# Six graph layers on one core: seven products for layer 2's queries, late copies of turned rows, one product moved, and thirteen stores on another queue

## The chip, the cores and the metric

The kernel runs on one core of a Trainium2 chip. The metric is the time of one execution on the device in microseconds (us), the median of several runs. One execution was also recorded by the hardware profiler; its records give a line, an engine, a start and a duration for every instruction. Durations quoted here come from that one execution. PE is the matrix engine, DVE the vector engine, ACT the scalar engine, POOL is GpSimd, and SP is the engine that issues most transfers. A queue such as SPq is the sequencer of an engine[...].

## The reference

A graph has N = 3327 nodes with 256 features each and a dense 0/1 adjacency matrix. Four residual layers are applied, each followed by a layer norm; the fourth holds three attention layers, which makes six stages in the kernel. Cut to what matters:

```python
# layer 0: cosine attention
Qn = cos_normalize(x @ Wq.T); Kn = cos_normalize(x @ Wk.T)
att = softmax(where(adj > 0, Kn @ Qn.T, NEG), axis=1)
x = layernorm(x + 0.5 * mask_of_empty_rows(att @ x, x) + 0.5 * x)
# layer 1: graph attention (GAT)
h = x @ W
e = leaky_relu(h @ a[:D] + (h @ a[D:]).T)
x = layernorm(x + elu(softmax(where(adj > 0, e, NEG)) @ h))
# layer 2: dot-product attention
q, k, v = x @ Wq.T + bq, x @ Wk.T + bk, x @ Wv.T + bv
x = layernorm(x + elu(softmax(where(adj > 0, q @ k.T / 16, NEG)) @ v))
# layer 3: h = x @ W0, then three GAT layers (3a, 3b, 3c), residual, layernorm
```

The adjacency matrix masks every attention. The kernel holds the weights transposed: a tile e has 128 nodes that are looked at on the partitions and 512 nodes that look along the columns, and the sum over neighbours is a matrix product that accumulates over the 26 row tiles.

## The kernel before

The nodes are padded to 3328, which is NT = 26 tiles of 128 rows. The columns fall into NB = 7 blocks: six of 512 columns (four tiles) and a last one of 256 (two tiles). The work is one long list of steps (layer, block b, tile j), 26 x 7 steps for each of the six layers in the order 0, 1, 2, 3a, 3b, 3c. Layers 1, 3a, 3b and 3c are GAT layers.

**A step.** `make` creates the weights of a step three steps ahead (`make_to`, LA): ACT computes an exponential or the two parts of the leaky form, DVE multiplies by the mask, and the result is the tile `e`. Then PE multiplies the e tile with the values of tile j and accumulates in `po`, which takes four PSUM banks for a full block and two for the last. A plain step does this with one 257-column product for each column tile (L1432). A block for which `strassen` is true (layer 2, and blocks 1 to 5 of layer 0) takes its steps in pairs and uses seven half-size products in place of eight; `sums` makes four combinations of the two e tiles on DVE, `combine` makes four combinations of the values once for each pair and stores them in DRAM (L713, through SP's queue), and `fetch_tsum` loads them again.

**The end of a block.** `finish` is a generator in `pending`; `advance()` takes it one step forward in each of the following steps, so that the end of block b is interleaved with the beginning of block b+1. In a GAT layer it scales the rows (`p4`, L1026), and `turn` (L827) transposes them: ACT separates the 32-bit rows into two planes of 16-bit halves (L834), SP issues one transposing DMA, the generator lets some steps pass (`turn_steps`, L848), and DVE copies the two planes back into place (L844). Then PE projects the rows with the weights of the layer (`pproj`, L1062), and exponential linear unit, residual and layer norm follow. The blocks before the last but one are projected by `projected4`, which uses seven products too, with four combined weights in `wsum`, spare columns of `FT[NB - 1]`. So the separate products of L1062 are found only in blocks NB-2 and NB-1. The scaled values of block NB-2 are turned during the last block, and those of the last block during the first steps of the next layer.

**The queries of layer 2.** `block2(b)` (L515) multiplies the transposed features of block b with a 256x256 matrix G (four 512-column products L522 in two `pgq` banks), adds a bias on ACT (L529), and takes a bound of the scores: a reduction on DVE (L537) and the product `pn` over the partitions (L545). The main loop starts it ahead of the block through `pre = ahead(nl, nb)` at step `begin` = 14 and takes it forward once a step. So block 0 of layer 2 is prepared in the last steps of layer 1, and it needs the rows that `finish` has just made.

**What sets the order.** The instructions are written in one program order. A scheduler that is entered at the start and closed after the first steps orders what each engine gets, by data dependence and by its own costs; every engine then runs its list in order. Tiles come from pools with a fixed number of buffers: e has five, `tsums` three, the tag `stage` (adjacency rows, turned planes, p4, x4) four, and the small PSUM pool for ps, pgq, pproj, pv and pn has three banks. An instruction that takes a buffer waits for its former readers.

**Layer 0, block 0** also reads the adjacency matrix as 32-bit numbers (L424), turns it into masks (ACT L435, L436), counts rows (DVE L449, L460; PE `pasum` L464), and normalises the keys of the next block on POOL (`kss`, `rs_*`, `rk`, L308 and L137 to L160), whose result DVE L379 and ACT L390 use. The thirteen stores of L713 for layer 0 fall into it.

The line of the plain product, before the change:

```python
for k in range(len(pos)):
    nc.tensor.matmul(pos[k], es[:, k * P : (k + 1) * P],
                     V[L.i % 2][j], start=(j == 0), stop=(j == NT - 1))
```

Of the kernel before, what the change touches and what calls it, by code (L numbers as in the profile page):

```python
# [8 lines left out]
F32 = mybir.dt.float32  # L9
# [4 lines left out]
AF = mybir.ActivationFunctionType  # L14
ALU = mybir.AluOpType
# [4 lines left out]
P = 128  # L20
D = 256
H = 128
# [11 lines left out]
def gnn_stack(ctx: ExitStack, tc: tile.TileContext, a: dict, N: int, out: bass.AP):  # L34
# [8 lines left out]
    nc = tc.nc  # L43
    NT = (N + P - 1) // P
    NP = NT * P
    NB = (NP + CH - 1) // CH
# [3 lines left out]
    def bw(b):  # L50
        return min(CH, NP - b * CH)
# [7 lines left out]
    cols = ctx.enter_context(tc.tile_pool(name="cols", bufs=2))  # L59
    mpool = ctx.enter_context(tc.tile_pool(name="mpool", bufs=2))  # L60
    work = ctx.enter_context(tc.tile_pool(name="work", bufs=2))
# [4 lines left out]
    def bank(name):  # L66
# [4 lines left out]
    start = tc.manual_schedule(  # L71
        engines={engines.PE, engines.Activation, engines.DVE, engines.Pool}
    )
# [9 lines left out]
    n = 8  # L83
# [9 lines left out]
    for k in range(4):  # L93
# [5 lines left out]
    V = [  # L99
        [big.tile([P, D + 1], F32, name=f"v{i}_{t}") for t in range(NT)]  # L100
        for i in range(2)
    ]

    FT = [big.tile([P, 2, CH], F32, name=f"ft{g}") for g in range(NB)]
# [6 lines left out]
    t_d = {  # L111
        k: [dram.tile([P, 4 * H + 1], F32, name=f"t{k}_d{p}") for p in range(NT // 2)]
        for k in ("0", "2")
    }
# [397 lines left out]

    gq = {}

    def block2(b):  # L515

        wd = bw(b)
        g = work.tile([P, 2, CH], F32, tag="x4k", name="gT", bufs=2)
        for o in range(2):
            pm = bank("pgq")  # L520
            for h in range(2):
                nc.tensor.matmul(  # L522
                    pm[:, :wd],
                    w["G"][:, h, o * P : (o + 1) * P],
                    FT[b][:, h, :wd],
                    start=(h == 0),
                    stop=(h == 1),
                )
            nc.scalar.activation(  # L529
                g[:, o, :wd], pm[:, :wd], AF.Identity, bias=w["u"][:, o : o + 1]  # L530
            )
            yield

        gm = cols.tile([P, 2], F32, tag="gm", name="gm")
        nc.vector.tensor_reduce(  # L537
            gm, g[:, :, :wd], AX.X, ALU.max, apply_absolute_value=True
        )
        nc.vector.tensor_tensor(gm, gm, gm, ALU.mult)  # L540
        g1 = cols.tile([P, 1], F32, tag="g1", name="g1")
        nc.vector.tensor_tensor(g1, gm[:, 0:1], gm[:, 1:2], ALU.add)
        yield
        pn = bank("pn")
        nc.tensor.matmul(pn[:, :1], ones, g1, start=True, stop=True)  # L545
        yield
        n2 = cols.tile([P, 1], F32, tag="n2", name="n2")
        nc.vector.tensor_scalar(n2, pn[:, :1], TINY, None, ALU.max)
        off = cols.tile([P, 1], F32, tag="off", name="off")
        rsqrt(off, n2, 1)  # L550
        nc.vector.tensor_tensor(off, off, n2, ALU.mult)
        nc.vector.tensor_scalar(off, off, -1.0, 80.0, ALU.mult, ALU.add)
        nc.vector.tensor_scalar(off, off, 0.0, None, ALU.min)
        gq[b] = g, off
# [135 lines left out]
    def combine(key, p, v, e=None):  # L690


        b1, b2 = v[2 * p], v[2 * p + 1]
        b11, b12, b21, b22 = b1[:, H:D], b1[:, :H], b2[:, H:D], b2[:, :H]
        if (key, p) in kept or key == "0":
            t = work.tile([P, 4 * H + 1], F32, tag="tsum", name="tsums", bufs=3)
        else:
            t = work.tile([P, 4 * H + 1], F32, tag="x4k", name="tsum", bufs=2)
        if (key, p) in kept:
            tsums[kept[key, p], p] = t  # L700
        t1, t2, t3, t4 = (t[:, c : c + H] for c in (0, H + 1, 2 * H + 1, 3 * H + 1))
        if e is None:
            nc.gpsimd.memset(t[:, H : H + 1], 1.0)
            nc.vector.tensor_tensor(t1, b12, b11, ALU.subtract)
            nc.vector.tensor_tensor(t3, b22, b12, ALU.subtract)
        else:
            one = t[:, H : H + 1]
            nc.vector.tensor_scalar(one, e[:, :1], 0.0, None, ALU.is_ge)
            nc.vector.scalar_tensor_tensor(t1, b12, one, b11, ALU.mult, ALU.subtract)
            nc.vector.scalar_tensor_tensor(t3, b22, one, b12, ALU.mult, ALU.subtract)  # L710
        nc.vector.tensor_tensor(t2, b22, t1, ALU.subtract)
        nc.vector.tensor_tensor(t4, t2, b21, ALU.subtract)
        nc.sync.dma_start(t_d[key][p], t)  # L713

    def fetch_tsum(key, b, p):
        t = work.tile([P, 4 * H + 1], F32, tag="tsum", name="tsums", bufs=3)
# [107 lines left out]
        return z[:, : 2 * q]  # L824


    def turn(x4, n, out, steps=3):  # L827

        half = "p k (n t) -> p t k n"
        pl = work.tile([P, 4, 2, D], U16, tag="x4k", name="planes", bufs=2)
        for t in range(2):
            nc.scalar.copy(pl[:, :n, t, :], x4[:, :n, :].bitcast(U16).rearrange(half, t=2)[:, t])  # L834
        yield
        tr = work.tile([P, 16, P], U16, tag="stage", name="turned", bufs=4)
        nc.sync.dma_start_transpose(
            out=tr[:, : 4 * n, :], in_=pl[:, :n].rearrange("p k t n -> p (k t n)")
        )
        for _ in range(steps):  # L840
            yield
        trv = tr[:, : 4 * n, :].rearrange("p (k t h) i -> p t k h i", t=2, h=2)
        for t in range(2):
            nc.vector.tensor_copy(out(t), trv[:, t])  # L844
        yield

    def turn_steps(L, b):

        if L.key == "1":
            return 5 if b == NB - 2 else 3  # L850
        return (9 if L.key == "3c" else 7) if b == NB - 2 else 4

    wsum = [
        FT[NB - 1][:, i // 2, D + (i % 2) * H : D + (i % 2 + 1) * H] for i in range(4)
    ]

    def sum_weights(wt):  # L860
        b11, b12, b21, b22 = (wt[:, h, o * H : (o + 1) * H] for h in range(2) for o in range(2))
# [72 lines left out]
    def finish(L, b, pos):  # L934
# [76 lines left out]
        else:  # L1011
# [25 lines left out]
            if L.key != "2":  # L1037
                pT4 = work.tile([P, 4, 2, P], F32, tag="x4k", name="pT4", bufs=2)
                yield from turn(
                    p4,  # L1040
                    n,
                    lambda t: pT4[:, :n].bitcast(U16).rearrange(
                        "p k h (i t) -> p t k h i", t=2
                    )[:, t],
                    turn_steps(L, b),
                )
                pTs = {k: pT4[:, k] for k in range(n)}
                if b < NB - 2:
                    c4 = work.tile([P, 4, D], F32, tag="x4k", name="c4", bufs=2)
                    yield from projected4(pT4, w[L.w], c4)  # L1050
# [304 lines left out]
    for s, (L, b, j) in enumerate(steps):  # L1355
# [43 lines left out]
        if end:  # L1399

            k, h = divmod(2 * j, NT)
            for i in (h, h + 1):
                for o in range(2 if k else 1):
                    e = made[i][:, k * P : (k + 1) * P]
                    nc.tensor.matmul(  # L1405
                        pos[1 + o][:, :P] if k else pos[0],
                        V[1][i][:, o * H : (o + 1) * H] if k else e,
                        e if k else V[1][i],
                        start=(i == 0),
                        stop=(i == NT - 1),  # L1410
                    )
            if j == 0:
                xm = fetch_last()

            if j == 9:
                esum = work.tile([P, D], F32, tag="ejunk", name="esum", bufs=2)[:, :P]
                nc.vector.tensor_tensor(esum, made[0][:, P:D], made[1][:, P:D], ALU.add)
            elif 9 < j < 22:
                for i in (2 * j - 18, 2 * j - 17):
                    nc.vector.tensor_tensor(esum, esum, made[i][:, P:D], ALU.add)  # L1420
            elif j == 23:
                pn = bank("pnlast")
                nc.tensor.matmul(pn[:, :1], esum, ones[:, :1], start=True, stop=True)
                rlast = cols.tile([P, 1], F32, tag="ri3", name="ri3")
                row_sums(pn[:, :1], rlast)
            if j == NT // 2 - 1:
                ends.append(finish_last(pos[0], xm, 0))
            if ends:
                next(ends[0], None)
        elif not strassen(L, b):  # L1430
            for k in range(len(pos)):
                nc.tensor.matmul(  # L1432
                    pos[k],
                    es[:, k * P : (k + 1) * P],
                    V[L.i % 2][j],
                    start=(j == 0),
                    stop=(j == NT - 1),
                )
        elif j % 2:
            products(pos, b, j // 2, es, V[L.i % 2])  # L1440
# [24 lines left out]
        if nb == NB:  # L1465
            nl, nb = (None if last else layers[L.i + 1]), 0
        begin = 2 if last and b == NB - 2 else 14
        if L.is_gat and (b, j) == (0, 22):
            sum_weights(w[L.w])
        if j == (25 if L.key == "1" else 22) and not end:  # L1470
# [87 lines left out]
```

## Time and profile before

| | us |
|---|---|
| median of 3 runs | 2356.33 (2355.39 to 2357.3) |
| the profiled execution, whole | 2355.78 |
| its span, first to last record | 2354.0 |
| one full block of layer 2 (905 to 994) | 89.0, of which DVE busy 56.9, ACT 22.6 |

The profiled execution is 0.55 us under the median, and 1.78 us of it lie outside the span. On PE every product leaves two records, so that a count of records is twice the count of products. The durations of single PE records overlap; what a product costs is the distance from start to start. In the stretches without waits that distance is, for one record, 0.429 us at 512 columns, 0.217 at 257, 0.216 at 256 and 0.112 at 128 or 129, and so for a product 0.858, 0.433, 0.431 and 0.223 us.

A line of the timeline gives start, length, engine, line, operation, names and the number of records that were merged. In brackets is the idle time of the engine ahead of it and what ended that.

### The profile page before, as it was taken

The page shows a single profiled execution, that of the slowest core. Times are in us where ns is not written, and L with a number is a line of the kernel's source. Part 1 is how long each engine was busy: PE and PEld are TensorE (multiplying, and loading weights), DVE is VectorE, ACT ScalarE, POOL GpSimd, SP SyncE. Part 2 cuts the span into 40 slices and gives each one's busy share as a digit, 9 for nine tenths or more (in the row PEclk, how much of TensorE's full clock was granted, in tenths as well). Part 3 has the DMA queues.
Part 4 walks back from the last instruction along what each step waited for, and adds up shares of the span by engine and source line. Part 5 has one row for each costly group of instructions (what it writes and reads, how often), then busy time and mean ns, then how long its engine had stood idle before and what let it go on. Part 6 is the DMA issues. An engine that isn't in the chain of part 4 may idle for free.

```text
span 2354.0 us, 33990 instructions
## 1 busy us (share of the span) xinstructions
PE 2335.3 (99%) x12257; PEld 1917.4 (81%) x12257; DVE 1665.8 (71%) x4500; ACT 1221.5 (52%) x1976; POOL 40.0 (2%) x156
## 2 busy tenths in 40 slices
PE   9999999999999999999999999999999999999997
PEld 6788888888888777767677798888888888888887
DVE  7789999867777666567567586666756666666676
ACT  4667777755555422222222255565665555655554
POOL 0000000000000000000000000000000000000000
PEclk9999999999999999999999999999999999999999
DMA  8655555423222312212212221210211111132111
GB/s 275 196 187 184 167 199 191 151 75 83 74 81 60 108 54 88 79 54 86 76 46 74 83 88 48 73 56 26 71 53 43 43 51 52 50 101 70 61 44 46
DMA packets 147293, 214.72 MB, mean 91 GB/s; under 512 B 76093, under 2 KB 101172, under 8 KB 142516
## 3 DMA queue, kind: packets, MB, share of 16 engines
q1 hardware_dynamic: 146852, 212.28, 28.1%
q8 instruction: 96, 1.57, 0.3%
q14 instruction: 73, 0.60, 0.1%
q10 hardware_dynamic: 272, 0.26, 0.0%
HBM read 167.53 MB, written 28.19 MB: 83 GB/s over the span
## 4 chain that ended last, share of the span: by engine, by line
PE 94%; DVE 3%; ACT 1%; DMA 1%; issue 1%; POOL 0%; SPq 0%; POOLq 0%; DVEq 0%; ACTq 0%
PE po L1432 48%; PE po L779 19%; PE ps L563 12%; PE ps L492 6%; PE pproj L890 3%; PE po L1405 1%; PE pv L1148 1%; PE pgq L522 1%; ACT re L657 1%; DMA stage<-in_adj_a 1%; PE pk L353 0%; DMA turned<-planes 0%; PE pq L317 0%; DVE e L668 0%; PE pproj L1062 0%
## 5 line engine op out<-in xcount | busy, mean ns | idle before, releaser
L1432 PE MATMUL po<-v,e 128*128 128x257 f32 x5616 | 1248.6, 381 | 1.5 <-ACT p L1026 1.3
L1432 PEld LDWEIGHTS po<-v,e 128*128 128x128 f32 x5616 | 1057.7, 190 | 165.3 <-issue 9.3
L657 ACT ACTIVATE re<-u,nrh,th 128x512 f32<-128x512 f32 (+1 forms) x728 | 556.1, 780 | 483.9 <-DVE e L668 478.0
L668 DVE SCALAR_TENSOR_TENSOR e<-re,rh,mask 128x512 f32<-128x512 f32 (+1 forms) x702 | 501.2, 718 | 347.6 <-PE po L1432 311.6
L563 PE MATMUL ps<-gT,ft 128*128 128x512 f32 (+1 forms) x728 | 307.4, 563 | 0.0
L571 ACT ACTIVATE ex<-ps,off 128x512 f32<-128x512 f32 (+1 forms) x182 | 119.1, 655 | 356.6 <-PE ps L563 356.0
L779 PE MATMUL po<-tsums,ssum 128*128 128x128 f32 (+1 forms) x1794 | 249.3, 275 | 0.0
L477 DVE SCALAR_TENSOR_TENSOR e<-ex,mask 128x512 f32<-128x512 f32 (+1 forms) x182 | 118.6, 651 | 164.1 <-ACT ex L571 163.3
L563 PEld LDWEIGHTS ps<-gT,ft 128*128 128x128 f32 x728 | 132.0, 190 | 114.5 <-issue 111.7
L779 PEld LDWEIGHTS po<-tsums,ssum 128*128 128x128 f32 x1794 | 224.5, 192 | 0.7 <-ACT y L982 0.3
L779 PEld LDWEIGHTS po<-v,e 128*128 128x128 f32 x1196 | 169.3, 191 | 67.4 <-issue 54.7
L779 PE MATMUL po<-v,e 128*128 128x129 f32 x1196 | 182.4, 275 | 0.0
L505 ACT ACTIVATE ex<-ps,rq 128x512 f32<-128x512 f32 (+1 forms) x183 | 118.7, 651 | 116.8 <-PE ps L492 107.5
L492 PE MATMUL ps<-ft,ft 128*128 128x512 f32 (+1 forms) x312 | 142.5, 561 | 0.0
L506 DVE SCALAR_TENSOR_TENSOR e<-ex,mask 128x512 f32<-128x512 f32 (+1 forms) x183 | 116.8, 644 | 34.2 <-ACT ex L505 33.2
L449 DVE CUSTOM_DVE_ANT_0 acc<-acc,stage 128x1024 uint16<-128x1024 uint16 (+1 forms) x168 | 108.7, 647 | 12.3 <-DMA stage<-in_adj_a 9.2
L779 PE MATMUL po<-tsums,e 128*128 128x128 f32 x598 | 92.3, 275 | 0.4 <-DVE y L821 0.4
L779 PE MATMUL po<-v,ssum 128*128 128x128 f32 x598 | 92.3, 275 | 0.0
L436 ACT ACTIVATE mask<-pos 128x1024 uint8<-128x1024 bf16 (+1 forms) x87 | 86.4, 993 | 2.1
L435 ACT ACTIVATE pos<-stage 128x1024 bf16<-128x1024 int32 (+1 forms) x87 | 85.6, 984 | 1.2 <-DVE e L506 1.2
L779 PEld LDWEIGHTS po<-tsums,e 128*128 128x128 f32 x598 | 79.3, 192 | 0.6 <-issue 0.6
L779 PEld LDWEIGHTS po<-v,ssum 128*128 128x128 f32 x598 | 79.4, 192 | 0.1
(295 smaller groups left out, 1899.7 us busy)
## 6 DMA issues: line engine op xcount, KB each, us to landing
mask<-mask_d SPq DMA_DIRECT2D x30, 1664.0 KB
stage<-in_adj_a SPq DMA_DIRECT2D x78, 512.0 KB
tsums<-t_d SPq DMA_DIRECT2D x152, 256.5 KB
mask_d<-mask SPq DMA_DIRECT2D x6, 1664.0 KB
u<-s_d SPq DMA_DIRECT2D x24, 256.0 KB
xT<-in_xT SPq DMA_DIRECT2D x10, 512.0 KB
mask<-mask_d SPq DMA_DIRECT2D x5, 832.0 KB
t_d<-tsums SPq DMA_DIRECT2D x14, 256.5 KB
```

The lines of the kernel that those rows point to most:

```text
L436: nc.scalar.activation(mask(b, j, 2), t_[:, : 2 * wd], AF.Sign)
L449: nc.vector.tensor_tensor(acc, acc, st[:, h * wd : (h + 1) * wd], ALU.add)
L477: nc.vector.scalar_tensor_tensor(e[:, :wd], t_[:, :wd], 0.0, mask(b, j), ALU.add, ALU.mult)
L492: nc.tensor.matmul(ps[:, :wd], FT[j // 4][:, 0, (j % 4) * P : (j % 4 + 1) * P], FT[b][:, 1, :wd], start=True, stop=True,)
L505: nc.scalar.activation(t_[:, c], ps[:, c], AF.Exp, scale=rq[:, j : j + 1])
L506: nc.vector.scalar_tensor_tensor(e[:, c], t_[:, c], 0.0, mask(b, j)[:, c], ALU.add, ALU.mult)
L563: nc.tensor.matmul(ps[:, :wd], FT[j // 4][:, h, (j % 4) * P : (j % 4 + 1) * P], g[:, h, :wd], start=(h == 0), stop=(h == 1),)
L571: nc.scalar.activation(t_[:, :wd], ps[:, :wd], AF.Exp, bias=off, scale=1.0 / D**0.5)
L657: nc.scalar.activation(t_[:, :wd], self.u[b][:, :wd], AF.Relu, bias=self.nrh[:, j : j + 1], scale=self.th[:, j : j + 1],)
L668: nc.vector.scalar_tensor_tensor(e[:, :wd], t_[:, :wd], self.rh[:, j : j + 1], mask(b, j), ALU.add, ALU.mult,)
L779: nc.tensor.matmul(o, x, y, start=(p == 0 and g not in banks[:i]), stop=(p == NT // 2 - 1 and g not in banks[i + 1 :]),)
L1432: nc.tensor.matmul(pos[k], es[:, k * P : (k + 1) * P], V[L.i % 2][j], start=(j == 0), stop=(j == NT - 1),)
```

## The change

Four parts:

1. `block2` computes the queries with seven 128x256 products in place of four 128x512 ones. Four combinations of G (`sum_G`) are made once, in layer 1 at block 6, j = 4, in the columns of `wsum`. Four combinations of the features (`gsums`) and eight additions of 128x256 for each block go to DVE, and ACT evicts two 128x256 tiles. Three PSUM banks are taken in place of two, the generator has four steps in place of two ahead of the reduction, and `begin` becomes 12 for layer 2.
2. The stores of `combine` for layer 0 are issued by GpSimd and no longer by SP.
3. In `turn`, block NB-2 of layers 1, 3a and 3b waits longer (7 and 8 steps in place of 5 and 7), and its two copies become `tensor_scalar` additions of a per-partition number `nought`, which is computed as "less than 0" from the newest e tile. It is 0 always, but the copies can't be ordered ahead of that tile.
4. In block 0 of layers 3b and 3c the product of the fourth column tile in step j = 0 is issued in step j = 1, after the first three of that step.

```diff
--- before.py
+++ after.py
@@ -512,24 +512,68 @@
 
     gq = {}
 
+
+
+    wsum = [
+        FT[NB - 1][:, i // 2, D + (i % 2) * H : D + (i % 2 + 1) * H] for i in range(4)
+    ]
+
+    def sum_G():
+
+        a11, a12, a21, a22 = (
+            w["G"][:, h, o * P : (o + 1) * P] for o in range(2) for h in range(2)
+        )
+        s1, s2, s3, s4 = wsum
+        nc.vector.tensor_tensor(s3, a11, a21, ALU.subtract)
+        nc.vector.tensor_tensor(s1, a21, a22, ALU.add)
+        nc.vector.tensor_tensor(s2, s1, a11, ALU.subtract)
+        nc.vector.tensor_tensor(s4, a12, s2, ALU.subtract)
+
     def block2(b):
 
+
         wd = bw(b)
+        q = wd // 2
+        add, sub = ALU.add, ALU.subtract
+        x = work.tile([P, 4, D], F32, tag="stage", name="gsums", bufs=4)
+        t1, t2, t3, t4 = (x[:, i, :q] for i in range(4))
+        b11, b12, b21, b22 = (FT[b][:, h, i * q : (i + 1) * q] for h in range(2) for i in range(2))
+        nc.vector.tensor_tensor(t1, b12, b11, sub)
+        nc.vector.tensor_tensor(t3, b22, b12, sub)
+        nc.vector.tensor_tensor(t2, b22, t1, sub)
+        nc.vector.tensor_tensor(t4, t2, b21, sub)
+        yield
+        a11, a12, a21, a22 = (
+            w["G"][:, h, o * P : (o + 1) * P] for o in range(2) for h in range(2)
+        )
+        s1, s2, s3, s4 = wsum
         g = work.tile([P, 2, CH], F32, tag="x4k", name="gT", bufs=2)
-        for o in range(2):
+        c11, c12, c21, c22 = (g[:, o, i * q : (i + 1) * q] for o in range(2) for i in range(2))
+
+        def two(*pairs):
             pm = bank("pgq")
-            for h in range(2):
-                nc.tensor.matmul(
-                    pm[:, :wd],
-                    w["G"][:, h, o * P : (o + 1) * P],
-                    FT[b][:, h, :wd],
-                    start=(h == 0),
-                    stop=(h == 1),
-                )
-            nc.scalar.activation(
-                g[:, o, :wd], pm[:, :wd], AF.Identity, bias=w["u"][:, o : o + 1]
-            )
-            yield
+            for i, (l, r) in enumerate(pairs):
+                nc.tensor.matmul(pm[:, i * q : (i + 1) * q], l, r, start=True, stop=True)
+            return pm[:, :q], pm[:, q : 2 * q]
+
+        m1, m2 = two((a11, b11), (a12, b21))
+        m6, m7 = two((s2, t2), (s3, t3))
+        yield
+        for o, c in enumerate((c12, c22)):
+            nc.scalar.activation(c, m1, AF.Identity, bias=w["u"][:, o : o + 1])
+        nc.vector.tensor_tensor(c11, c12, m2, add)
+        nc.vector.tensor_tensor(c12, c12, m6, add)
+        nc.vector.tensor_tensor(c22, c22, m6, add)
+        nc.vector.tensor_tensor(c21, c22, m7, add)
+        m5, m4 = two((s1, t1), (a22, t4))
+        yield
+        nc.vector.tensor_tensor(c12, c12, m5, add)
+        nc.vector.tensor_tensor(c22, c21, m5, add)
+        nc.vector.tensor_tensor(c21, c21, m4, sub)
+        m3, _ = two((s4, b22))
+        yield
+        nc.vector.tensor_tensor(c12, c12, m3, add)
+        yield
 
 
 
@@ -710,7 +754,7 @@
             nc.vector.scalar_tensor_tensor(t3, b22, one, b12, ALU.mult, ALU.subtract)
         nc.vector.tensor_tensor(t2, b22, t1, ALU.subtract)
         nc.vector.tensor_tensor(t4, t2, b21, ALU.subtract)
-        nc.sync.dma_start(t_d[key][p], t)
+        (nc.gpsimd if key == "0" else nc.sync).dma_start(t_d[key][p], t)
 
     def fetch_tsum(key, b, p):
         t = work.tile([P, 4 * H + 1], F32, tag="tsum", name="tsums", bufs=3)
@@ -824,7 +868,7 @@
         return z[:, : 2 * q]
 
 
-    def turn(x4, n, out, steps=3):
+    def turn(x4, n, out, steps=3, late=False):
 
 
 
@@ -840,22 +884,25 @@
         for _ in range(steps):
             yield
         trv = tr[:, : 4 * n, :].rearrange("p (k t h) i -> p t k h i", t=2, h=2)
-        for t in range(2):
-            nc.vector.tensor_copy(out(t), trv[:, t])
+        if late:
+
+            e = next(m for m in reversed(made) if m is not None)
+            nought = cols.tile([P, 1], F32, tag="nought", name="nought")
+            nc.vector.tensor_scalar(nought, e[:, :1], 0.0, None, ALU.is_lt)
+            for t in range(2):
+                nc.vector.tensor_scalar(out(t), trv[:, t], nought, None, ALU.add)
+        else:
+            for t in range(2):
+                nc.vector.tensor_copy(out(t), trv[:, t])
         yield
 
     def turn_steps(L, b):
 
         if L.key == "1":
-            return 5 if b == NB - 2 else 3
-        return (9 if L.key == "3c" else 7) if b == NB - 2 else 4
-
-
-
-
-    wsum = [
-        FT[NB - 1][:, i // 2, D + (i % 2) * H : D + (i % 2 + 1) * H] for i in range(4)
-    ]
+            return 7 if b == NB - 2 else 3
+        return (9 if L.key == "3c" else 8) if b == NB - 2 else 4
+
+
 
     def sum_weights(wt):
         b11, b12, b21, b22 = (wt[:, h, o * H : (o + 1) * H] for h in range(2) for o in range(2))
@@ -1043,6 +1090,7 @@
                         "p k h (i t) -> p t k h i", t=2
                     )[:, t],
                     turn_steps(L, b),
+                    b == NB - 2 and L.key != "3c",
                 )
                 pTs = {k: pT4[:, k] for k in range(n)}
                 if b < NB - 2:
@@ -1428,13 +1476,20 @@
             if ends:
                 next(ends[0], None)
         elif not strassen(L, b):
-            for k in range(len(pos)):
+            todo = [(es, j, k) for k in range(len(pos))]
+
+            if L.key in ("3b", "3c") and b == 0:
+                if j == 0:
+                    held = todo.pop()
+                elif j == 1:
+                    todo.insert(3, held)
+            for e, i, k in todo:
                 nc.tensor.matmul(
                     pos[k],
-                    es[:, k * P : (k + 1) * P],
-                    V[L.i % 2][j],
-                    start=(j == 0),
-                    stop=(j == NT - 1),
+                    e[:, k * P : (k + 1) * P],
+                    V[L.i % 2][i],
+                    start=(i == 0),
+                    stop=(i == NT - 1),
                 )
         elif j % 2:
             products(pos, b, j // 2, es, V[L.i % 2])
@@ -1465,6 +1520,10 @@
         if nb == NB:
             nl, nb = (None if last else layers[L.i + 1]), 0
         begin = 2 if last and b == NB - 2 else 14
+        if nl is not None and nl.key == "2":
+            begin = 12
+        if L.key == "1" and (b, j) == (NB - 1, 4):
+            sum_G()
         if L.is_gat and (b, j) == (0, 22):
             sum_weights(w[L.w])
         if j == (25 if L.key == "1" else 22) and not end:
```

## The prediction

> **What bounds the kernel now.** I read the page first: the busy time of the engines, the chain that ended last, the costliest group.
>
> ```profile
> PE 2335.3 (99%) x12257; PEld 1917.4 (81%) x12257; DVE 1665.8 (71%) x4500; ACT 1221.5 (52%) x1976; POOL 40.0 (2%) x156
> ...
> PE 94%; DVE 3%; ACT 1%; DMA 1%; issue 1%; POOL 0%; SPq 0%; POOLq 0%; DVEq 0%; ACTq 0%
> ...
> L1432 PE MATMUL po<-v,e 128*128 128x257 f32 x5616 | 1248.6, 381 | 1.5 <-ACT p L1026 1.3
> ```
>
> PE is the bound nearly throughout. Time is won only by taking products away or by closing a gap of PE. The second view, the waits of PE, says how little the gaps hold:
>
> ```profile
> PE pasum L464 <- DVE af L460: 1.8, 2, 1.1
> PE po L1432 <- ACT p L1026: 1.3, 2, 0.7
> ...
> PE pproj L1062 <- DVE pT L844: 0.3, 1, 0.3
> ```
>
> The third view is the timeline of PE where the change acts: the start of layer 2's preparation, the two changes from one GAT layer to the next, the end of layer 0's first block.
>
> ```profile
> 784.93 1.99 PE L1062 MATMUL pproj<-w_l_w,pT 128*128 128x256 f32 x8
> ```
>
> ```profile
> 1706.73 6.55 PE L1432 MATMUL po<-v,e 128*128 128x257 f32 x29 [0.66 <-ACT p L1026]
> ```
>
> ```profile
> 2024.25 8.07 PE L1432 MATMUL po<-v,e 128*128 128x257 f32 x36 [0.65 <-ACT p L1026]
> ```
>
> ```profile
> 93.76 0.63 PE L464 MATMUL pasum<-ident,af 128*128 128x128 f32 x4 [1.12 <-DVE af L460]
> ```
>
> Measured from start to start beyond the usual distance, PE loses 0.82 us at each of 1706.73 and 2024.25, 1.29 at 93.76, 0.22 at 784.93 and 0.23 and 0.43 at the pproj of the two later GAT ends (1687.50, 2005.03). Fourth, the windows view for one block of layer 2, with columns for PE, PEld, DVE, ACT and POOL:
>
> ```profile
> 905.00:994.00 89.00, 89.00 (x481) 62.19 (x480) 56.90 (x163) 22.58 (x38) 0.00 (x0) 1.00 0.25 77
> ```
>
> PE has no idle time at all there, DVE and ACT have room. Last, the groups by shape, for prices on DVE (busy time, then mean ns):
>
> ```profile
> L844 DVE COPY pT<-turned 128x1024 uint16<-128x1024 uint16 x48 | 32.9, 740 | 3.0 <-DMA turned<-planes 3.0
> ...
> L1118 DVE TENSOR_SCALAR o<-y,st,rstd 128x256 f32<-128x256 f32 x50 | 17.4, 409 | 0.5
> ...
> L1079 DVE TENSOR_SCALAR z<-c 128x256 f32<-128x256 f32 x40 | 9.0, 288 | 0.3
> ```
>
> L1118 takes its two factors per partition from memory, L1079 has constants in the instruction. Same size, same type, both in on-chip memory: 409 against 288 ns. Back to back, four of L1118 take 1.38 us in the chain (796.50), 0.345 us each.
>
> [...]
>
> **Part 1, seven products.** Before, a full block has four products of 0.858 = 3.43 us (eight records of 0.429). After, seven of 0.431 = 3.02. That is 0.415 less. The half block goes from four of 0.431 to seven of 0.223: 0.16 less. Blocks 1 to 5 and the half block lie inside layer 2: 5 x 0.415 + 0.16 = 2.24 us saved on PE, where PE is never idle, so all of it counts unless DVE comes late. DVE gets four combinations and eight additions of 128x256, at 0.34 back to back: 4.1 us. It has 89.0 - 56.9 = 32 us free, but it works in order. After a block's end it runs without a gap for about 25 us (1083 to 1108) and is still 3.5 us ahead of the products that need it; in the new instruction order about 1.4 us of the additions fall before that point, which leaves 2.1. In the quiet part of a block it idles 2.8 us for each pair of steps. Hence cost nothing; the cover is that lead. sum_G's four small instructions (0.28 each) lie in layer 1, where DVE waits for PE: nothing.
>
> The end of layer 1 is different, since block 0's queries need rows that are only just made. In the chain, the way runs from the pT copies (784.76) through pproj, elu, norm (o, 796.50) and gm (797.88) to pn (800.00). Between the norm and gm now stand the eight additions in turn with products and evictions, and the norm itself is later for being interleaved; I count the first score tile about 6 us later, ACT and DVE work included. The first product of layer 2 comes at 816.28, the scores of its first tile at 804.23, so most of it is covered. What is left, by stepping through the new order with the trace's durations, is 0.73 us ahead of the first pair of layer 2 and 0.15 at its pv products, against 0.28 at pn before: +0.60. With the 0.415 saved here too: +0.18 without the late copies.
>
> **Part 3, late copies.** A pair of L844 copies takes 1.37 us from the first's start to the second's end. As `tensor_scalar` with a per-partition number it either keeps that[...]: 1024 x 0.345/256 = 1.38 less L1118's fixed part, about 1.1 each, 2.3 for the pair. That is between 0 and +0.9, with 0.16 for `nought`, a small instruction. L1118 is the only comparable row, so I take the slow rate, +1.0 together. What does it hit? The three places have pproj waiting for pT already (0.22, 0.23, 0.43 us). There is no cover left, and pproj stays where it was at the end of layer 1 and comes one product (0.43, of which some 0.2 is used) later in the other two. So the pT stall becomes 1.15 (+0.93), about 1.0 (+0.77) and 1.2 (+0.77).
>
> The landing of the turned planes (DMA 3.6 to 3.9 us in the chains) comes no later for it: in the new order of DVE the copies stand behind one or two more e tiles, but those need no more than the wait for the landing leaves idle anyway.
>
> **Part 4, the held product.** At 1706.73 and 2024.25 the fourth tile waits for p, 0.82 us each. Held over the next step's first three products it comes 1.3 us later, and p comes earlier as well because two fewer of the new layer's e tiles are ahead of it on DVE. Both stalls go: -0.82 each. What is late next is the first e of the new layer: both u activations (0.71 each) now stand ahead of its first exponential part on ACT. Its slack was about 1.0 us, less the 0.6 of the second one that used to stand behind; I count +0.2 each. With the pT stalls each boundary is -0.82 + 0.77 + 0.2 = +0.15.
>
> **Part 2, the stores.** On SP thirteen issues of 0.33 us and their waits go. SP's last wait of this kind (83.91, 2.76 us) ends right ahead of the issue at 86.76 of the adjacency rows that PE's 1.29 us depend on (landing 91.2). But this load also needs a buffer, and ACT's L435 frees it only at 85.03 + 1.05 = 86.08. At most 0.6 us can come of it; I take -0.5. On POOL the stores are queued with the chain for rk (64.01 to 69.42): in the new order the store of d10 (data at 67.06) stands between kss and rs_g, d11's (69.68) two instructions on. At 1 us each rk ends at about 74.3 in place of 69.42. DVE L379 (71.70) waits for it, with an e behind; ACT L390 and the next exponential (73.08) wait too, and that e is then ready at 76.6 in place of 74.47. PE needs it at about 78.8: 2.2 us left, nothing lost. Free stores leave it as it is; from 2 us a store on, each us more costs PE up to two.
>
> **The sum.** Layer 2 -2.24; end of layer 1: 0.93 + 0.60 - 0.415 = +1.1; two GAT boundaries +0.3; layer 0 -0.5. Together -1.3 on the profiled execution's 2355.78 (span 2354.0 and 1.78 around it): 2354.4. The median lies 0.55 higher; a prediction of the next median could be as much above.
>
> **Rivals.** *The late copies keep their rate.* Then the 0.93 and the two 0.77 go: end of layer 1 +0.2, boundaries -0.62 each, sum -2.24 + 0.2 - 1.24 - 0.5 = -3.8; with all of the e delay gone too, -4.4. Time 2351.4 to 2352.0. For it: the copies are 16-bit[...]; against it: L1118.
>
> *Nothing is gained.* Every saving on PE is given back as new waits at the block starts of layer 2 (0.4 us each suffices), layer 0 gains nothing: the boundaries' +1.8 remain, about 2358. For it: DVE works in order and is loaded at each start of a block; against it: the 2.1 us of lead.
>
> *Slower.* One mechanism: in each block of layer 2 the additions of part 1 wait, in DVE's order, for products that PE does late (a product issued behind a pair's 28, 3.12 us) and for ACT's evictions, and hold e and sums behind them. The place is the three groups of additions. It decides from the point at which a wait exceeds the lead of 2.1 us: 1.0 us at two of the three groups in six blocks are +12, less the 1.3: 2367. For it: in-order DVE at 64% of these blocks; against it: `block2` issues a group's products one step of the loop (half a pair, 3.3 us) ahead of its additions.
>
> **How the numbers follow.** A difference under about 0.2% (4.7 us) can't be told from none. My forecast, -1.3, has 0.48 (2352.5 to 2357); copies at full rate 0.24 (2350 to 2352.5), of which about two thirds would be faster by over 0.2%; nothing gained 0.13 (2357 to 2361, no change); slower 0.15 (from 2361). Some 0.04 more of faster for savings that I don't see. Faster 0.20, same 0.65, slower 0.15. The range, 2350 to 2360.5, takes in the first three cases with the bounds of the copies' rate and of the stores.
>
> **What would show it.** Right: in layer 2's blocks PE stays without idle time and a full block takes 88.6; the rows of L844's place show two `tensor_scalar` of about 1.1 us each; PE's waits list pproj on pT with about 1 us each in place of p; pasum's wait falls by half. Wrong: copies of 0.74 us (the second case); waits of L779 or L563 for DVE or ACT in every block of layer 2 (the slower one); ACT L390 waiting for POOL with PE idle at 75 to 82 (the stores).

## The result and the profile after

The changed kernel takes 2362.1 us in the median of 13 runs, the kernel before 2356.1 in runs beside it: ratio 1.0025, 95% interval 1.0017 to 1.0033. One of the 13, at 10728 us, was a slow run and is left out of the ratio; the median of the other twelve is 2361.7. The change makes the kernel slower by about 6 us; forecast was a time of 2354.4, 1.3 us less than before. The profiled execution took 2364.25 us with a span of 2362.1, so it shows about 2 us more than the median; against the 2354.0 of before it has 8.1 us to explain.

The page again, busy times and chain:

```profile
PE 2335.8 (99%) x12299; PEld 1925.4 (82%) x12299; DVE 1688.8 (71%) x4591; ACT 1217.8 (52%) x1976; POOL 45.1 (2%) x169
...
PE 93%; DVE 3%; DMA 2%; ACT 1%; issue 1%; POOL 0%; POOLq 0%; DVEq 0%; ACTq 0%
```

PE's busy time should have dropped by 2.7 us and has risen by 0.5. The waits of PE (total in us, times, longest):

```profile
PE pv L1196 <- DVE ft L896: 3.2, 1, 3.2
PE pasum L464 <- DVE af L460: 2.9, 3, 1.2
PE pproj L1110 <- DVE pT L893: 1.9, 3, 0.8
PE pn L329 <- ACT ft L325: 1.3, 1, 1.3
...
PE po L1487 <- DVE e L712: 1.0, 2, 0.5
```

The two waits for p are gone. Those for `pasum` and `pproj` have grown, and waits at `pv`, at `pn` and for e are new. Where the time went is seen by lining up the same products of both traces (block sums, row products, the first product of a projection) and taking the difference of their starts. The stretches are in the time of the trace before:

| stretch | after minus before, us | foretold |
|---|---|---|
| layer 0 (to 468) | +3.6 | -0.5 |
| layer 1's last steps and layer 2's first block and a half (767 to 872) | +5.3 | +0.7 |
| rest of layer 2 | -1.8 | -1.8 |
| 3a to 3b | +0.1 | +0.15 |
| 3b to 3c | +0.3 | +0.15 |
| the end of 3c | +0.6 | 0 |

The second row's forecast is the +1.1 less 0.4 for block 1, whose queries fall into this stretch.

**Layer 2** is as foretold: the difference falls by 0.41 us in each full block and 0.16 in the half one, and PE has no idle time. The windows view of one block (length, PE, PEld, DVE, ACT, POOL, clock):

```profile
1005.00:1093.50 88.50, 88.50 (x486) 63.30 (x485) 60.16 (x175) 22.35 (x38) 0.00 (x0) 1.00 0.23 73
```

**Layer 0.** The timeline of POOL (start, length, what):

```profile
63.76 0.54 POOL L757 DMA_DIRECT2D t_d<-tsums  x1 [2.03 <-DVE tsums L756]
72.06 0.25 POOL L308 TENSOR_SCALAR kss<-kss 128x4 f32<-128x4 f32 x1 [7.76 <-ACT ex L505]
72.28 0.74 POOL L757 DMA_DIRECT2D t_d<-tsums  x1
```

`kss` starts 8 us later than before (64.01), although ACT had its operand ready at 64.18. The view of line 308 has the reason, in before and then in after:

```profile
L308 POOLq MODIFY_POOL_CONFIG  x2: 6/6/6, 3.1 to 3.1; - x2
```

```profile
L308 POOLq MODIFY_POOL_CONFIG  x2: 37/37/37, 64.4 to 64.4; - x2
```

In both traces the first arithmetic on POOL is preceded by a change of its configuration. Before, POOL got to it at 3.1 us and nobody noticed. Now it is queued behind seven stores, and 7.6 us pass between it and kss. A store itself takes 0.54 us there. POOL's result rk comes at 77.1, and ACT, on which L390 stands ahead of the next exponential, is idle for 6.21 us until then:

```profile
77.34 0.69 ACT L390 ACTIVATE ft<-ft,rk 128x128 f32<-128x128 f32 x2 [6.21 <-DVE rk L379]
```

PE then waits 0.5 us for the next exponential and 1.3 us for the copy of L325, which both stand behind this on ACT.

The 3.6 us are those of one execution. In the traces of three experiments below with the stores in the same place (e4, e9, e10; kss at 71.5 to 72.3) 2.4 to 2.8 us are lost between 60 and 132 us, but only 0.5 to 1.4 of that are left at 468. Here nothing was won back.

**The start of layer 2.** SP's timeline before, then after:

```profile
796.94 1.82 SPq L1130 DMA_DIRECT2D x_d<-o  x4
799.98 1.60 SPq L837 DMA_TRANSPOSE turned<-planes  x1
802.61 0.33 SPq L409 DMA_DIRECT2D mask<-mask_d  x1
```

```profile
806.36 0.33 SPq L409 DMA_DIRECT2D mask<-mask_d  x1
807.86 1.88 SPq L1178 DMA_DIRECT2D x_d<-o  x4
811.03 4.86 SPq L881 DMA_TRANSPOSE turned<-planes  x1
```

The rows o are later, so the load of the next mask (1664 KB) is issued ahead of their transposition, which then takes 7.57 us to land (chain of waits of after), where before the first copy of the landed rows began 3.7 us after the issue:

```profile
811.03 7.57 DMA turned<-planes
...
818.62 1.37 DVE ft L896 x2
```

From start to start PE loses 3.4 us at pv (3.2 in the list of waits), and that is not the end of it. The windows after the wait:

```profile
820.00:822.00 2.00, 1.96 (x5) 1.64 (x6) 0.09 (x1) 0.00 (x0) 0.02 (x1) 0.58 0.00 0
822.00:824.00 2.00, 2.00 (x7) 1.56 (x7) 1.01 (x3) 0.00 (x0) 0.00 (x0) 0.57 0.00 0
824.00:826.00 2.00, 2.00 (x9) 1.51 (x8) 1.59 (x6) 0.00 (x0) 0.00 (x0) 1.00 0.00 0
```

The granted clock (the seventh figure) is 0.58 and 0.57 here. The pv records follow each other at 0.427 us in place of 0.216 for 3.4 us: another 1.8 us, counted as busy. So this wait costs 5.2 in this execution.

**The copies and the transpositions.** Groups by shape:

```profile
L896 DVE COPY pT<-turned 128x1024 uint16<-128x1024 uint16 x42 | 28.8, 740 | 11.5 <-DMA turned<-planes 11.5
...
L893 DVE TENSOR_SCALAR pT<-turned,nought 128x1024 uint16<-128x1024 uint16 x6 | 4.4, 795 | 2.9 <-DMA turned<-planes 2.9
```

A late copy takes 795 ns, not 1100: it keeps nearly the rate of the plain one. But the plain copies of the other blocks now wait 11.5 us for their transposed planes, where they waited 3.0. The view of the tile `turned` (minimum, median, maximum in ns), before and after:

```profile
L837 SPq DMA_TRANSPOSE turned<-planes x34: 1238/1616/2127, 519.6 to 2317.5; - x34
```

```profile
L881 SPq DMA_TRANSPOSE turned<-planes x34: 1238/1844/4864, 523.2 to 2325.0; - x34
```

The transpositions have become slower, also in code that the change does not touch. In the undisturbed blocks the first copy now begins 4.3 us after the issue, where it was 3.75.

### The profile page after: what moved, and what is told of

It reads as the page before. It is cut to its first block, busy times and chain, and to the rows that moved or that the text cites. A ratio compares the mean times of both kernels' runs of the same rounds, so it can differ in the third digit from the quotient of the medians.

```text
span 2362.1 us, 34167 instructions
## 1 busy us (share of the span) xinstructions
PE 2335.8 (99%) x12299; PEld 1925.4 (82%) x12299; DVE 1688.8 (71%) x4591; ACT 1217.8 (52%) x1976; POOL 45.1 (2%) x169
## 4 chain that ended last, share of the span: by engine, by line
PE 93%; DVE 3%; DMA 2%; ACT 1%; issue 1%; POOL 0%; POOLq 0%; DVEq 0%; ACTq 0%
PE po L1487 49%; PE po L823 19%; PE ps L607 12%; PE ps L492 5%; PE pproj L937 3%; PE pv L1196 1%; PE pgq L556 1%; DMA stage<-in_adj_a 1%; DMA turned<-planes 1%; PE pproj L1110 1%; PE po L1453 1%; PE pk L353 0%; PE pq L317 0%; ACT re L701 0%; DVE e L712 0%
```

## The experiments

Every time is a median, and every ratio is taken against runs of the kernel before on the same chip, whose median is 2355.4 in all three series (it was 2356.1 beside the changed kernel). So the times are best compared by their distance to before: +6.0 us for the changed kernel. Its own runs spread from 2359.9 to 2364.3 us, so what an edit gives back is uncertain by about 1 us either way. The runs are named e1 to e14 (e3 and e6 do not occur). The theories that their expectations name by letters are ones about this loss: A, POOL's configuration; B, GpSimd's queue slows the transpositions; C, the mask load; D, where the tiles lie; E, the additions of part 1 make the rows late.

### POOL: the stores back on SP, the configuration first, the stores alone

```diff
-        (nc.gpsimd if key == "0" else nc.sync).dma_start(t_d[key][p], t)
+        nc.sync.dma_start(t_d[key][p], t)
```

> The changed kernel with the thirteen stores of layer 0 back on SP's queue. Theory A (the stores push POOL's one-time configuration, about 7.6 us between 64.4 and 72.06, onto the path of rk): layer 0's 3.5 us come back, about 2358.5, kss at about 64 again. Rival A' (the stores' own time on POOL, 0.54 to 0.87 us each): the same time, so this run alone does not tell the two apart. Theory B (a transposing transfer takes longer, 1.84 in place of 1.62 us on SP, because GpSimd's queue is in use): the transposing issues are back at 1.62 us and the wait of pproj in layer 3c's end, where nothing was changed, is gone. Rival B' (chance of one execution): still 1.8 or anything between. The wait of 3.2 us for ft at the start of layer 2 stays in every theory, or shrinks a little.

e1: 2357.74 us, ratio 1.0010 (1.0003 to 1.0017); kss starts at 64.5, and layer 0 ends 0.8 us behind before in place of 3.6. But the median transposition stays at 1.86 us. The distance to before is 2.3 us, so the stores on GpSimd's queue cost 3.7 us, and they are not what slows the transpositions: theory B is wrong.

```diff
+    warm = cols.tile([P, 4], F32, tag="warm", name="warm")
+    nc.gpsimd.memset(warm, 1.0)
+    nc.gpsimd.tensor_scalar(warm, warm, 1.0, None, ALU.max)
```

> The changed kernel with one small maximum on POOL (a 128x4 tile of ones) at the very start, so that POOL is configured at about 3 us as in the kernel before, the stores still on GpSimd's queue. Theory A: kss starts at about 64 although seven stores stand ahead of it; 2.5 to 3.5 us come back, about 2359. Rival A' (the stores' own time in the queue): under 1 us comes back, above 2361. Theory B: the transposing issues stay at 1.84 us, since GpSimd still issues the stores.

e2: 2359.45 us, 1.0016 (1.0009 to 1.0023): +4.0, which is 2.0 less than the changed kernel with the stores where they were. In this trace layer 0 ends 0.3 us behind before in place of 3.6. POOL's timeline of this run:

```profile
64.62 0.54 POOL L757 DMA_DIRECT2D t_d<-tsums  x1 [2.03 <-DVE tsums L756]
65.23 0.21 POOL L308 TENSOR_SCALAR kss<-kss 128x4 f32<-128x4 f32 x1
```

kss comes 0.07 us after the seventh store's end. The first operation waits at the start of the kernel instead (view of the line of the new maximum):

```profile
L1374 POOLq MODIFY_POOL_CONFIG  x2: 11/11/11, 2.8 to 2.8; - x2
L1374 POOL TENSOR_SCALAR warm<-warm x1: 371/371/371, 13.6 to 13.6; 128x4 f32<-128x4 f32 x1
```

That is the price by itself: 10.8 us there, where nobody needs POOL. In the new order two stores (d10, d11) also stand behind rk, so a part of the gain may be theirs. The configuration accounts for 2.0 of the 3.7 us; what the other 1.7 are stays open.

This trace shows one thing more. PE waits at pv nearly as long as in the changed kernel:

```profile
PE pv L1196 <- DVE ft L896: 3.1, 1, 3.1
```

But the granted clock stays at 1.00, the pv records follow at 0.216 us, and the stretch from 767 to 872 costs 1.8 us less than in the changed kernel. So the loss through the clock doesn't come with every such wait.

> The kernel before with one part of the change alone: the thirteen stores of layer 0 through GpSimd's queue. Theory A (POOL's configuration of about 7.6 us falls behind the stores and onto rk's path): kss at about 72, 2.5 to 4 us more than before, all of it before 130 us of the trace, the transpositions at 1.62 us. Rival A'' (the loss of layer 0 in the changed kernel came from the other order of SP and ACT there): kss at about 64 and under 1 us.

e5: the edit is the first one of this section, the other way round and in the kernel before. 2357.5 us, 1.0008 (0.9999 to 1.0016), just inside no change. Its trace shows kss at 73.2, configuration at 65.9, and 3.6 us lost by the end of layer 0 with the transpositions at 1.61. The median loses 2.1, less than the 2.5 to 4 expected, and its profiled execution (2359.2) is the longest of all 13. That execution lost time to the clock as well: PE's waits on ACT were followed by half the clock from 82.7 to 86.1 us, which is 1.7 of the 3.6. Theory A holds for the mechanism, which this trace shows without the rest of the change; the size differs from execution to execution.

### The 64 bytes

The tile `nought` lies in a pool ahead of the masks and of the work pool. With two buffers it moves all their tiles up by 64 bytes per partition. In the program before, every tile `planes` and `turned` begins on a multiple of 256 bytes within a partition (the first `turned` at 167680); in the changed one they all begin 64 bytes past one. I took this as a new theory, D, after the first runs.

```diff
+    for _ in range(2):
+        nought = cols.tile([P, 1], F32, tag="nought", name="nought")
+        nc.gpsimd.memset(nought, 0.0)
```

> The kernel before, with nothing of the change but a 128x1 tile 'nought' with its two buffers in the same pool, set once at the start and never read: it moves the masks and all tiles of the work pool up by 64 bytes per partition, as in the changed kernel. Theory D (transposing transfers are slower where their tiles don't begin on a multiple of 256 bytes; before they do, in the changed kernel they begin 64 bytes past one, with the small tile at the start of POOL 128): the median issue of a transposition on SP rises from 1.62 to about 1.85 us, pproj waits 0.2 to 0.5 us longer at three places, the time rises by 0.5 to 1.5 us. Rival D' (it is the late copies that slow them, by what runs beside them): 1.62 us and the time of before.

e8: 2359.16 us, 1.0017 (1.0010 to 1.0024): 3.8 us for a tile that no one reads, in a kernel that is otherwise the one before. That is far more than the 0.5 to 1.5 expected. The tile `turned` and the waits of PE:

```profile
L837 SPq DMA_TRANSPOSE turned<-planes x34: 1237/1838/2027, 519.6 to 2320.3; - x34
```

```profile
PE pproj L1062 <- DVE pT L844: 3.5, 4, 1.5
...
PE po L1436 <- ACT p L1026: 1.3, 2, 0.7
```

The wait of pproj rises from 0.3 to 3.5 us, at four places, with copies that were not changed. Between the two traces these places lose 0.6, 1.0, 1.3 and 0.4 us, which is nearly all of the difference.

```diff
-            nought = cols.tile([P, 1], F32, tag="nought", name="nought")
+            nought = cols.tile([P, 32], F32, tag="nought", name="nought")[:, :1]
```

> The changed kernel with the tile 'nought' made 128 bytes wide, of which one column is used, so that everything behind it moves by 256 bytes in place of 64. Theory D: transpositions back at 1.62 us, the waits of pproj at 0.2 to 0.5 us, 1 to 2 us less than the changed kernel's 2362. Rival D': 1.85 us and no difference.

e9: 2359.68 us, 1.0019 (1.0012 to 1.0026): +4.3, so 1.7 less than the changed kernel, by moving its tiles another 192 bytes.

```profile
L881 SPq DMA_TRANSPOSE turned<-planes x34: 1237/1607/5153, 522.0 to 2322.1; - x34
```

The late copies are still there, and their waits, 1.9 us in the changed kernel, are not (waits of PE):

```profile
PE pproj L1110 <- DVE pT L893: 0.2, 1, 0.2
```

So theory D holds from both sides for the shifts tried, though its size was not foreseen. A shift of 128 bytes is slow too: the early maximum above moved the tiles to 128, and its median is 1824 ns. Which tile has to lie well, source or destination, was not tried, and the masks move with them.

### The late copies and the mask load

```diff
-                    b == NB - 2 and L.key != "3c",
...
-            return 7 if b == NB - 2 else 3
-        return (9 if L.key == "3c" else 8) if b == NB - 2 else 4
+            return 5 if b == NB - 2 else 3
+        return (9 if L.key == "3c" else 7) if b == NB - 2 else 4
```

> The changed kernel with the copies of block NB-2 as before (plain copies, 5 and 7 steps). Theory C (the mask load of the next block now stands ahead of the transposition of layer 1's block 5 on SP and fills the transfer engines): here the mask load stands behind it again, so the 3.2 us wait of pv for ft goes: about 2359. Rival C' (the eight additions make the rows late by themselves): pv still waits 2 us or more, about 2361. If the late copies cost time in themselves, another 1 to 2 us go at the three pproj.

e4: 2358.33 us, 1.0012 (1.0006 to 1.0019): +2.9. This does not tell theory C from its rival, because I had read the order of SP wrongly: the mask load stands behind the four stores of o, but still ahead of the transposition. The landing took 9.79 us and pv waited 3.3. The run takes away the late copies and, with them, the small tile. The transpositions are back at 1.61 us, which is the tile's part. The two waits of PE for e (1.0 us by the view, 0.66 each from start to start) are gone as well; in e9, which keeps the late copies, they were still there, so they belong to the late copies. 3a to 3b becomes 1.0 us shorter than before.

> The changed kernel with block 0 of layer 2 prepared by the four products of before, the other blocks by seven. Here too the mask load stands behind the transposition on SP, but the late copies stay. Theory C: the pv wait goes, less the 0.4 us of products: about 2359. Rival C'' (the late copies make the rows late): pv still waits 2 us or more, about 2361.

e7: 2362.31 us, 1.0033 (1.0020 to 1.0045). Here too the mask load is ahead of the transposition (landing 8.47 us, pv waits 2.1), so nothing of it is regained; its profiled execution, the longest of the five, loses 7.3 us in layer 0 with the stores on POOL, 3.4 of them to half the clock between 81.9 and 88.7 us. The expectation missed: the run tells only that four products alone do not restore the order.

```diff
+        if after:
+            nc.vector.tensor_scalar(
+                m[:, :1], FT[NB - 2][:, 0, :1], 0.0, None, ALU.is_ge
+            )
         nc.sync.dma_start(m[:, : NT * bw(b)], mask_d[b])
```

> The changed kernel, in which the mask load of layer 2's block 1 must wait: one column of its tile is written first from the transposed rows of block 5, and the load overwrites that. So the load can't stand ahead of the transposition of these rows. Theory C (the load fills the transfer engines): the landing of the planes at the start of layer 2 falls from 7.6 to about 4.3 us and pv's wait for ft from 3.2 us to under 0.5; about 2359. Rival C' (rows are late by themselves): pv waits 2.5 us or more, about 2362.

e10: 2359.05 us, 1.0017 (1.0011 to 1.0024): +3.7, so 2.3 less than the changed kernel; between the traces the stretch from 767 to 879 is 2.9 shorter. SP issues the load 7.8 us behind the transposition, which lands in 5.27 us (chain of waits):

```profile
809.22 5.27 DMA turned<-planes
814.51 0.74 DVE ft L900
815.25 0.31 DVE ssum L777
815.61 0.94 PE po L827 x6
```

The wait does not vanish, it is 1.9 us from start to start, now for `ssum`, which stands between the two copies on DVE. The clock stays at 1.00 and the pv records follow at 0.216 us. So both are right in part: the load cost 2.3 us in the median and 2.9 between these two traces, of which 1.8 are the clock's, and the rows are late by themselves, by what is left of the wait.

### Putting the gains together

> Seven products, the held product and the delayed mask load, but copies of block NB-2 as before (no shift by 64 bytes) and the stores back on SP's queue. If the four costs found (POOL's configuration 3.6, mask load 3, shift and late copies 2 us together) are the whole loss, what is left are the gains: 2.2 us of products in layer 2 and about 1 us at the two GAT boundaries, so 3 us under the kernel before, about 2352.5. If another cost hides behind them: within 1 us of before.

e11: the edits are those above, delayed mask load, plain copies, stores on SP. 2352.89 us, 0.9988 (0.9981 to 0.9994): 2.5 under before, as expected, and 8.5 less than the changed kernel. One by one the three edits gave 2.3, 3.1 and 3.7, together 9.1, so no large cost hides behind these.

```diff
-            if L.key in ("3b", "3c") and b == 0:
+            if False:
```

> The best version so far without the held product. If holding it is worth what its two waits were (0.82 us each): 1.0 to 1.6 us more, about 2354.3, with the two waits of po for p back. If the waits had gone by the other orders anyway: no difference.

e14: 2353.99 us, 0.9993 (0.9985 to 1.0002), 1.1 more. Between the two traces the boundaries 3a to 3b and 3b to 3c lose 1.6 us. The two waits are back (waits of PE):

```profile
PE po L1490 <- ACT p L1077: 1.3, 2, 0.6
```

> The best version so far (seven and held products, delayed mask load, plain copies, stores on SP) with block 0 of layer 2 prepared by four products. There PE waited 1.2 us for the turned rows of layer 1's block 5 because the norm that makes them shares DVE with the eight additions. Theory E: without the additions the wait goes, 0.4 us of products come back, 0.5 to 1 us less than the best version, about 2352. Rival E' (the step count, not the additions, sets when the rows are made): no difference or 0.4 us more.

e12: 2353.1 us, 0.9991 (0.9983 to 0.9999): no difference to the best version. The wait of pv is gone, and in its trace 0.9 us less are lost on the way into layer 2, but the transposition at 3b to 3c was issued for 3.4 us in this execution, and pproj waited 1.9 us for it. Theory E stays open in size.

> The best version so far with the stores on GpSimd's queue and POOL configured at the start, tiles moved by 256 bytes. If the stores' queue is worth anything in itself (SP's wait of 2.8 us ahead of the adjacency rows), layer 0 gets up to 0.6 us shorter: about 2352.3. If GpSimd's stores cost even with the configuration out of the way: 1 us or more above the best version.

e13: 2351.34 us, 0.9985 (0.9978 to 0.9991): the lowest median of all, 4.1 us under before. With POOL configured early and the tiles moved by 256 bytes, GpSimd's queue is no loss, and perhaps the gain of up to 0.6 that was foretold from SP's side; 1.5 us between two medians with ranges of 4 us do not settle it. In its trace kss is at 64.2 and layer 0 ends 1.0 us ahead of before.

## Why the prediction was wrong

**Part 1 in layer 2 was right.** 0.415 us for a full block and 0.16 for the half one, nothing for DVE: measured 0.41 and 0.16. The rival for the slower side (additions that hold up DVE in every block) did not happen.

**The end of layer 1 was wrong by 4.6 us**, nearly half of the miss. The step was "0.73 us ahead of the first pair of layer 2 and 0.15 at its pv products". I stepped through PE, DVE and ACT and left SP's queue out. The rows come later, as counted, but lateness changes what stands ahead of them there: the mask load passes the transposition, which then lands in 7.6 us in place of 3.7. PE waits 3.4 us, and in the profiled execution its clock halves after that, another 1.8. The delayed load takes back 2.3 to 2.9.

**Part 2 was wrong by 4.1.** "At 1 us each rk ends at about 74.3" put stores and arithmetic in one queue and priced the stores too high: the 1 us was an assumption, for in before every store of L713 is issued by SP, and 0.54 us is what the changed kernel shows. What I missed is the configuration, which stands in the list as an instruction without operands, right behind the seventh store. I gave it no time. rk ended at 77.1, ACT L390 waited for it, and the exponential and the copy behind it reached PE too late: the sign "ACT L390 waiting for POOL with PE idle at 75 to 82" came true. "2.2 us left, nothing lost" thus failed. The 4.1 is of one execution; in the medians the stores cost 3.7 (e1) or, alone, 2.1 (e5). Nor did the gain of 0.5 on SP's side show here: the waits of `pasum` rose from 1.8 to 2.9 us. The warning that I placed there, "from 2 us a store on, each us more costs PE up to two", had the place right and the cause wrong.

**Part 3 had a right number for a wrong reason.** The pT stalls were foretold as 1.15, 1.0 and 1.2 us and measured as 0.97, 0.52 and 0.91. But the copies are not slow: 795 ns beside the plain copy's 740, where I took 1100. That was an estimate from L1118's 345 ns for 256 numbers, less a fixed part that no row shows. L1118 differs in more than the scalar, it has 32-bit data and two factors. The stalls come from the 64 bytes by which the new small tile moves everything behind it: moved to 256, they are 0.2 us in all. The same shift explains the 0.4 us at the end of 3c, where nothing was changed. That cost was in no step; alone it is 3.8 us in the kernel before.

**Part 4 was right in mechanism.** The waits for p went, and holding the product is worth 1.1 us in the median and 1.6 between the traces (foretold 1.6, or 1.2 with the later e). "I count +0.2 each" for the first e was too small: 0.66 each, and without the late copies it is nothing. So it is a cost of part 3, not of part 4.

"Copies keep their rate" thus came true and its time did not, since the stalls it meant to remove had another cause. By its time the result falls into "Slower" (from 2361), whose mechanism, additions that hold up every block of layer 2, did not happen; "Nothing is gained" (about 2358) put the loss into the block starts of layer 2, where there is none.

## What to carry to other kernels

When a step becomes late, follow it through the transfer queues as well: what was behind it may pass it, and a big load ahead of a small urgent one holds it up (7.6 us to the landing here, 5.3 with the load behind); give the big one a dependence that keeps it behind. A new tile need not be free, however small: 64 bytes that no one reads cost 3.8 us here (e8), so look at what it moves. Before transfers are put in front of GpSimd's first arithmetic, let it do one small instruction of that kind at the start (2.0 us here, e2). And one trace is one execution: whether a wait also costs clock differed from run to run here (2.0 us at pv did in e1, 3.1 in e2 did not).

## What the runs showed of the hardware

- POOL's first arithmetic comes 7.6 us after its configuration at 64.4 (changed kernel), 7.3 us after it at 65.9 (e5), and 10.8 us after it when that is at 2.8 (e2). With stores on that queue the early one gave 2.0 us here.
- The issue of a transposing transfer takes 1.61 to 1.62 us in the median of 34 with the tiles where they are in the kernel before (before, e4) or 256 bytes further (e9), and 1.82 to 1.86 with them moved by 64 bytes (the changed kernel, e8, e1) or 128 (e2). At the four places where PE waits for the landing, e8 loses 0.4 to 1.3 us each.
- The length of a gap of PE alone does not decide whether its clock drops. In the changed kernel 3.2 us of waiting at pv were followed by half the clock from 820.32 to 823.73. After 2.0 us there e1 has 0.85, 0.50 and 0.80 of the clock in the three stretches of 2 us from 816 to 822. After 3.3 us e4 has 0.61 from 816.5 to 819 and 0.63 from 819 to 821, and after 3.6 us e9 has 0.55 from 820 to 822. But after 3.1 us e2 kept its full clock, and so did e10 after 1.7 at the product that waits for `ssum`. What does decide it was not shown.
